# Column-major edge tiles in a chain of four modulated convolutions, with the edge products, edge tables and first iterations reordered

## The chip, the cores and the metric

One core of a Trainium2 chip runs the kernel. The metric is the device time of one execution in microseconds, as the median of several runs.

## The reference

The input x has 128 rows of 64 channels and 1024 positions. Four layers follow each other, each a 3-tap convolution whose weights are scaled for every row by a style vector, and the result is added to x. Layers 0 and 2 keep the length, layer 1 doubles it and blurs, layer 3 blurs and halves it.

```python
def _layer(x, style, w, b, mw, mb, typ):
    s = style @ mw.T + mb
    weight = SCALE * w * s[:, None, :, None]
    demod = lax.rsqrt(jnp.sum(weight * weight, axis=(2, 3)) + EPS)
    weight = weight * demod[:, :, None, None]
    if typ == 'same':
        out = jax.vmap(_conv_same)(x, weight) + b[None, :, None]
    elif typ == 'upsample':
        out = jax.vmap(_conv_up)(x, weight.transpose(0, 2, 1, 3)) + b[None, :, None]
        out = _blur(out, 2.0 * blur_k, (1, 1))
    elif typ == 'downsample':
        xb = _blur(x, blur_k, (2, 2))
        out = jax.vmap(_conv_down)(xb, weight) + b[None, :, None]
    return out
...
for i, typ in enumerate(TYPES):          # same, upsample, same, downsample
    out = _layer(out, style, weights[i], biases[i], mod_w[i], mod_b[i], typ)
x = x + out
```

## The kernel before

Away from the two ends of a row, the four layers and the blurs are one 9-tap convolution with weights of the row's own. The kernel computes these 9 x 64 x 64 weights for each row and then applies them. It works on four rows at a time ("quad" q, 32 of them); the array of TensorE is used as four quarters of 64 x 64, so that a step is four matmuls, each in two passes (float32).

Weights of a quad: stage1 (tile S, PSUM psS), stage2 (tile R, psR) and stage3 (tile Wf, PSUM psA or psW) are small products; between them ScalarE or VectorE copies the PSUM out with a factor from a table for the row (tA, tB, tBn, tC, t0). stage1 is split in stage1_a and stage1_b from quad 4 on: stage1_a computes three blocks, two "ends" and one "middle"; four copies take them to S; GpSimd adds and subtracts (L473, L474); stage1_b writes more blocks to the same PSUM and VectorE makes the rest of S (L483). The middle products of neighbouring rows are shared (share, share_copy: ScalarE copies the shared block into psR, L533, before stage2 of the next quad).

Convolution: x comes as three planes, and the 9 taps are computed as five products of 3 taps each, 342 columns wide (L816, 12 matmuls, 24 records of the profile): conv3, conv1, conv2, conv4, conv0. Their inputs T are sums and differences of planes (VectorE L763, L714 G and L794, GpSimd L780 and L785), their weights H are sums of the taps (VectorE L714 H, L711). conv3, conv1, conv2 and conv0 use the PSUM tile psA of the quad, conv4 the tile Y. VectorE takes psA into Y and y between them (L714, L873), ScalarE writes the outputs o (L893), and SP's queue stores them. psA has two buffers: open_a(q + 1), whose first user is stage3_b, takes the buffer of psA[q - 1].

Ends: the first and last three positions of a row don't follow the 9-tap rule. They are computed for all rows at once, layer by layer, from x's ends (Xe): the edge tiles Xm, Ye, Ue, Ve, We and Oe hold, for two ends (or halves) and 64 rows (HB), 3 to 6 positions each. Before, a row's positions are neighbours in memory. ends_matmul (L1046) multiplies such a tile with the weights of a layer, into the PSUM tile psA[q - 1], free at that time; rest0 to rest3 on VectorE (L1076, L1099, L1129, L1160) read it into the next edge tile with a table's factor. This happens in turns q = 10, 11, 13 and 24 (SLOTS), ahead of conv2(q). The factors (s0h, a0r, c0r, a1h, c1h, b1h, Dar, c2r, times) and the bias terms (add0, rest1_inner, add2) are made by GpSimd, a few in each turn (TABLES).

The order on every engine is the order in which the code is written (manual schedule): a prologue, early_turn for q = 0 to 3, turn_of for q = 4 to 28, then the last three quads by hand. In early_turn, q = 3 prepares two quads ("twice"); q = 4 is the first turn_of ("entry"). SMALL adds tiny matmuls (L1323) into columns of Y that small_zeros clears first (memset L1316). POOL in the profile is GpSimd, DVE VectorE, ACT ScalarE, PE TensorE.

Of the kernel before, what the change touches and what calls it, by code (L numbers as in the profile page):

```python
# [55 lines left out]
K = 3  # L56
# [7 lines left out]
def kernel(  # L64
# [395 lines left out]
    def stage1_a(q, ps=None):  # L460
# [532 lines left out]
    Xm = const.tile([P, 2, HB, K], F32, name="Xm")  # L993
# [11 lines left out]
    def zeros():  # L1005
        for t in (Ve, We):
            for s in range(2):
                nc_g.memset(t[:, s, :, 5:6], 0.0)
# [31 lines left out]
    def ends_matmul(ps, n, moving, plan):  # L1040
        for i, (weight, src, dst) in enumerate(plan):
            for r, rows in enumerate(HALF):
                for c, cols in enumerate(HALF):
                    out_ = ps[r][cols, : HB * n].rearrange("c (b j) -> c b j", j=n)
                    d = dst(r) if callable(dst) else dst
                    nc.tensor.matmul(  # L1046
                        out_[:, :, d],
                        weight(r, c)[rows],
                        moving[rows, c, :, src],
# [5 lines left out]
    def in_psum(t, n):  # L1055
        return t[:, :, : HB * n].rearrange("c h (b j) -> c h b j", j=n)
# [18 lines left out]
    def rest0(t):  # L1075
        nc_v.tensor_tensor(Ye[:, :, :, 1:], in_psum(t, K), spread(a0r, K), op=ALU.mult)  # L1076
# [51 lines left out]
    def rest2(t):  # L1128
        nc_v.tensor_tensor(Ve[:, :, :, :5], in_psum(t, 5), spread(Dar, 5), op=ALU.mult)  # L1129

    def add2():
        dst = Ve[:, :, :, :2]
        nc_g.tensor_add(dst, dst, spread(c2r, 2))

    def blur_side(part, i):
# [3 lines left out]
            dst[:, :, bs, :5], src[:, :, bs, :5], src[:, :, bs, 1:], op=ALU.add  # L1139
# [17 lines left out]
    def rest3(t):  # L1157
        scale = td.rearrange("c q r -> c (q r)")[:, :, None].to_broadcast([P, HB, K])
        for e in range(2):
            nc_v.scalar_tensor_tensor(  # L1160
                Oe[:, :, e], in_psum(t, K)[:, e], 0.125, scale, op0=ALU.mult, op1=ALU.mult
# [190 lines left out]
    def last_factors():  # L1352
        for i, f in enumerate((2.0, -1.0, 3.0)):
# [6 lines left out]
        7: lambda: table_b(REST),  # L1360
        8: lambda: of_half(s0h, sc[:, 0]),
        9: lambda: (
            nc_g.tensor_mul(quads(a0r), by_half(dm[:, 1]), by_half(dm[:, 0])),
            nc_g.tensor_copy(quads(c0r), by_half(c0f)),
        ),
# [406 lines left out]
```

## Time and profile before

| | |
|---|---|
| median of 3 runs | 468.58 us (468.55 to 469.73) |
| the profiled execution, device time | 468.84 us |
| its span, first to last instruction | 467.0 us |
| TensorE busy | 461.9 us, 99% |
| VectorE busy | 426.4 us, 91% |
| ScalarE busy | 329.6 us, 71% |
| GpSimd busy | 195.7 us, 42% |
| mean granted TensorE clock | 0.999 of full speed |
| HBM | 35.03 MB read, 34.01 MB written |

The profile is one execution, 1.8 us of which lie around the span. A row of the timeline gives the start and length in us, engine, line of the kernel, operation, tiles written and read, shape and count, and in brackets the idle time before it with what ended that. Matmuls overlap, and their ends are modelled, so their rows overlap too and TensorE looks busy where it waits briefly.

### The profile page before, as it was taken

The page shows a single profiled execution, that of the slowest core. Times are in us where ns is not written, and L with a number is a line of the kernel's source. Part 1 is how long each engine was busy: PE and PEld are TensorE (multiplying, and loading weights), DVE is VectorE, ACT ScalarE, POOL GpSimd, SP SyncE. Part 2 cuts the span into 40 slices and gives each one's busy share as a digit, 9 for nine tenths or more (in the row PEclk, how much of TensorE's full clock was granted, in tenths as well). Part 3 has the DMA queues.
Part 4 walks back from the last instruction along what each step waited for, and adds up shares of the span by engine and source line. Part 5 has one row for each costly group of instructions (what it writes and reads, how often), then busy time and mean ns, then how long its engine had stood idle before and what let it go on. Part 6 is the DMA issues. An engine that isn't in the chain of part 4 may idle for free.

```text
span 467.0 us, 26805 instructions
## 1 busy us (share of the span) xinstructions
PE 461.9 (99%) x11906; PEld 387.2 (83%) x11906; DVE 426.4 (91%) x671; ACT 329.6 (71%) x817; POOL 195.7 (42%) x263
## 2 busy tenths in 40 slices
PE   9999999999999999999999999999999999999996
PEld 6988789878777777998997777778777899998973
DVE  4989998889999999899899999999999899999995
ACT  4576667688777778576887777787777687776554
POOL 4733233676455535444333434423343433445410
PEclk9999999999999999999999999999999999999999
DMA  5226555425444534455344545444454534454225
GB/s 179 95 94 202 157 155 180 155 98 182 153 154 155 185 121 159 126 162 179 124 154 139 170 156 185 152 152 143 152 173 156 182 117 159 147 182 156 94 93 185
DMA packets 52837, 70.78 MB, mean 152 GB/s; under 512 B 6129, under 2 KB 50929, under 8 KB 52721
## 3 DMA queue, kind: packets, MB, share of 16 engines
q1 hardware_dynamic: 52496, 68.84, 45.6%
q8 instruction: 93, 1.52, 1.4%
q14 instruction: 24, 0.19, 0.2%
q10 hardware_dynamic: 224, 0.23, 0.1%
HBM read 35.03 MB, written 34.01 MB: 148 GB/s over the span
## 4 chain that ended last, share of the span: by engine, by line
PE 96%; DVE 2%; issue 0%; ACT 0%; DVEq 0%
PE psA L816 46%; PE Y L816 12%; PE psR L513 10%; PE psA L623 7%; PE psW L623 7%; PE psS L430 5%; PE psR L591 4%; PE psA L513 1%; PE psA L1046 1%; PE Y L184 1%; DVE G L714 0%; DVE H L714 0%; PE Y L380 0%; ACT S L400 0%; PE psM L221 0%
## 5 line engine op out<-in xcount | busy, mean ns | idle before, releaser
L816 PE MATMUL psA<-T,H 64*64 64x342 f32 x2304 | 191.9, 449 | 0.0
L816 PEld LDWEIGHTS psA<-T,H 64*64 64x64 f32 x2304 | 107.9, 134 | 32.6 <-issue 1.0
L780 POOL TENSOR_TENSOR T<-G 128x688 f32<-128x688 f32 x28 | 47.0, 1677 | 77.9 <-DVE G L714 71.4
L714 DVE SCALAR_TENSOR_TENSOR G<-X 128x1378 f32<-128x1378 f32 (+2 forms) x65 | 78.4, 1212 | 0.1
L816 PE MATMUL psA<-T,Wf 64*64 64x342 f32 (+1 forms) x918 | 67.6, 404 | 0.0
L473 POOL TENSOR_TENSOR S<-S 128x128 f32<-128x128 f32 x28 | 14.3, 511 | 127.1 <-ACT S L400 127.1
L816 PE MATMUL Y<-T,Wf 64*64 64x342 f32 x768 | 63.7, 448 | 0.0
L400 ACT ACTIVATE psW<-psA 128x128 f32<-128x128 f32 x100 | 19.4, 269 | 53.3 <-PE psA L623 51.2
L794 DVE TENSOR_TENSOR T<-G 128x1376 f32<-128x1376 f32 (+1 forms) x34 | 52.1, 1532 | 0.0
L763 DVE TENSOR_TENSOR T<-X 128x688 f32<-128x688 f32 x32 | 51.1, 1596 | 0.0
L400 ACT ACTIVATE Wf<-psW,t 128x256 f32<-128x256 f32 (+2 forms) x76 | 32.7, 479 | 25.4 <-PE psW L623 24.6
L400 ACT ACTIVATE R<-psR,tC 128x448 f32<-128x448 f32 x63 | 36.5, 630 | 18.0 <-PE psR L591 12.8
L785 POOL TENSOR_TENSOR T<-G 128x688 f32<-128x688 f32 x28 | 48.0, 1714 | 0.0
L816 PEld LDWEIGHTS psA<-T,Wf 64*64 64x64 f32 x918 | 42.8, 133 | 4.6 <-issue 0.2
L816 PEld LDWEIGHTS Y<-T,Wf 64*64 64x64 f32 x768 | 37.3, 133 | 10.5 <-DVE Y L714 0.2
L430 PEld LDWEIGHTS psS<-wd,w2n 64*64 64x64 f32 x1344 | 37.9, 134 | 8.3 <-ACT S L400 1.0
L893 ACT ACTIVATE o<-psA,tb,td 128x342 f32<-128x342 f32 x63 | 36.9, 641 | 5.2 <-PE psA L816 5.2
L714 DVE SCALAR_TENSOR_TENSOR Y<-m,psA 128x684 f32<-128x684 f32 x31 | 27.1, 874 | 14.4 <-PE psA L816 14.1
L714 DVE SCALAR_TENSOR_TENSOR H<-Wf 128x384 f32<-128x384 f32 x64 | 39.5, 618 | 0.0
L893 ACT ACTIVATE o<-y,tb,td 128x342 f32<-128x342 f32 x62 | 39.1, 694 | 0.0
L513 PE MATMUL psR<-S,E 64*64 64x64 f32 (+1 forms) x1152 | 39.0, 235 | 0.0
L513 PEld LDWEIGHTS psR<-S,E 64*64 64x64 f32 x1152 | 36.9, 134 | 2.5 <-ACT psR L533 0.3
(193 smaller groups left out, 922.9 us busy)
## 6 DMA issues: line engine op xcount, KB each, us to landing
out<-o SPq DMA_DIRECT2D x191, 172.0 KB, 2.1
X<-in_x SPq DMA_DIRECT2D x150, 172.0 KB, 3.3
X<-in_x SPq DMA_DIRECT2D x14, 516.0 KB, 4.6
par<-in_params SPq DMA_DIRECT2D x3, 192.0 KB, 3.4
Xe<-in_x_ends SPq DMA_DIRECT2D x1, 192.0 KB, 2.8
out<-o ACTq DMA_DIRECT2D x1, 172.0 KB, 1.9
par<-in_params SPq DMA_DIRECT2D x1, 160.0 KB, 2.7
out<-Oc SPq DMA_DIRECT2D x1, 150.0 KB, 1.7
```

Source lines behind the costliest of these rows:

```text
L400: nc_a.activation(dst, src, AF.Copy, scale=f)
L430: nc.tensor.matmul(ps[r][cols, at * C : (at + n) * C], weight[rows], wd[c if r == 0 else 1 - c][rows, taps], start=first, stop=last, skip_ ...
L513: nc.tensor.matmul(dst[r][cols], weight[rows], st[c if r == 0 else 1 - c][rows, slots, :], start=False, stop=last, skip_group_check=True,)
L591: nc.tensor.matmul(ps[r][cols, lo * C : (lo + m) * C], E[rows, e + 2, :], src[rows, a, :], start=(n == 0), stop=(n == 8), skip_group_check ...
L623: nc.tensor.matmul(dst[r][cols], weight[rows], t[rows, c, slots, :], start=first, stop=last, skip_group_check=True,)
L714: nc_v.scalar_tensor_tensor(out, x, f, y, op0=ALU.mult, op1=op)
L763: nc_v.tensor_sub(t[:, pairs, 0, :NJ], plane(X, 3, pairs), plane(X, 1, pairs))
L780: eng.tensor_add(t[:, :, 0, :NJ], plane(g, 2), plane(g, 1))
L785: eng.tensor_sub(t[:, :, 1, :NJ], plane(g, 2), plane(g, 1))
L794: nc_v.tensor_sub(t[:, pairs, :, :NJ], both(a, PL), both(b, 1))
L816: nc.tensor.matmul(ps[s][cols, at], w, Ts[q, tag][rows, c, i, g + at.start : g + at.stop], start=(g == at.start == 0 and (m == 3 or alone) ...
L893: nc_a.activation(dst, src, AF.Identity, bias=add, scale=d3)
```

## The change

1. Edge tiles and the PSUM that the edge products write are laid out position by position (for each position, 64 rows in a line) where they were row by row. The instructions and their sizes stay.
2. In turns 10, 11, 13 and 24 the edge products stand behind the first two of three tap groups of conv2, not ahead of it.
3. From turn 7 on, GpSimd makes the edge tables behind the two S operations of the turn (BEHIND_S), not ahead of them; s0h moves from turn 8 to 7 and c1h from 10 to 9.
4. First iterations: at q = 1 small_zeros stands ahead of in1 and in2, and in_g01(c) behind stage1_b; at q = 3 and 4 the two copies of stage1's middle block go from ScalarE to VectorE (stage1_middle), at q = 4 later than the ends' copies.

TensorE at the edge products of turn 11 (Ye and g, weights of layer 1) and at stage3_b behind conv2, with the engines whose semaphores each row waits for; before:

```order
L513 MATMUL psR_1_3553<-S_3203,E 64x64 x2
L1046 MATMUL psA_3097<-Ye,g_166 64x64x2 [waits Activation_49]
L1046 MATMUL psA_3097<-Ye,g_166 64x64x2 x11
L1046 MATMUL psA_3097<-Ye,g_166 64x64x2 [waits Pool_49]
L1046 MATMUL psA_3097<-Ye,g_166 64x64x2 x3
L1046 MATMUL psA_3097<-Ye,g_166 64x64 x8
L816 MATMUL psA_3388<-T_11_3287,H_3099 64x342 [waits DVE_49]
L816 MATMUL psA_3388<-T_11_3287,H_3099 64x342 x11
L623 MATMUL psA_3689<-R_3636,w0s_155 64x192 [waits DVE_49,Activation_49]
```

and after:

```order
L519 MATMUL psR_1_3553<-S_3201,E 64x64 x2
L822 MATMUL psA_3385<-T_11_3289,H_3097 64x342 [waits DVE_49,Pool_49]
L822 MATMUL psA_3385<-T_11_3289,H_3097 64x342 x7
L1053 MATMUL psA_3095<-Ye,g_166 64x2x64 [waits Activation_49]
L1053 MATMUL psA_3095<-Ye,g_166 64x2x64 x11
L1053 MATMUL psA_3095<-Ye,g_166 64x2x64 [waits Pool_49]
L1053 MATMUL psA_3095<-Ye,g_166 64x2x64 x3
L1053 MATMUL psA_3095<-Ye,g_166 64x64 x8
L822 MATMUL psA_3385<-T_11_3289,H_3097 64x342 x4
L629 MATMUL psA_3686<-R_3636,w0s_155 64x192 [waits DVE_49,Activation_49]
```

Between the edge products and stage3_b's first row there were 12 matmuls of conv2, and there are 4. That row waits for VectorE (DVE) before and after; in turns without edge products it waits for ScalarE alone.

GpSimd from turn 8 to 10 (S: stage1's sums, T: conv1's and conv2's inputs, R: stage2's sums, then the tables); before:

```order
L333 TENSOR_SCALAR s0h<-sc 64x64 x2
L473 TENSOR_TENSOR S_2928<-S_2928 128x2x64
L474 TENSOR_TENSOR S_2928<-S_2928 128x2x64
L780 TENSOR_TENSOR T_10_3012<-G_2942 128x2x344
L640 TENSOR_TENSOR R_3070<-R_3070 128x2x128
L785 TENSOR_TENSOR T_10_3012<-G_2942 128x2x344
L1363 TENSOR_TENSOR a0r<-dm 128x128
L1364 COPY c0r<-c0f 128x128
L473 TENSOR_TENSOR S_3203<-S_3203 128x2x64
L474 TENSOR_TENSOR S_3203<-S_3203 128x2x64
L780 TENSOR_TENSOR T_11_3287<-G_3217 128x2x344
```

and after:

```order
L481 TENSOR_TENSOR S_2928<-S_2928 128x2x64
L786 TENSOR_TENSOR T_10_3012<-G_2942 128x2x344
L646 TENSOR_TENSOR R_3070<-R_3070 128x2x128
L791 TENSOR_TENSOR T_10_3012<-G_2942 128x2x344
L480 TENSOR_TENSOR S_3201<-S_3201 128x2x64
L481 TENSOR_TENSOR S_3201<-S_3201 128x2x64
L1371 TENSOR_TENSOR a0r<-dm 128x128
L1372 COPY c0r<-c0f 128x128
L333 TENSOR_SCALAR c1h<-cc_152 64x64 x2
L786 TENSOR_TENSOR T_11_3289<-G_3215 128x2x344
```

The tables of a turn went from ahead of the S rows to behind them, ahead of the T row of conv1.

VectorE in iteration q = 1 (memset of small_zeros, conv1's and conv2's inputs, and so on to G of the next quad); before:

```order
L780 TENSOR_TENSOR T_2_952<-G_928 128x2x344
L785 TENSOR_TENSOR T_2_952<-G_928 128x2x344
L1316 MEMSET Y 128x16
L794 TENSOR_TENSOR T_2_1005<-G_928 128x1376
L763 TENSOR_TENSOR T_3_1007<-X_103 128x688
L985 TENSOR_TENSOR cc_152<-Y,a_145 128x16
L988 SCALAR_TENSOR_TENSOR cc_152<-b1s,cc_152 128x16
L714 SCALAR_TENSOR_TENSOR y_2_1072<-psA_989,m_2_1002 128x684
L714 SCALAR_TENSOR_TENSOR G_1074<-X_103 128x2x689
L483 SCALAR_TENSOR_TENSOR S_1049<-psS_0_1035,tB,S_1049 128x192
L483 SCALAR_TENSOR_TENSOR S_1049<-psS_1_1036,tB,S_1049 128x192
L714 SCALAR_TENSOR_TENSOR G_1074<-X_103 128x2x344
```

and after:

```order
L1323 MEMSET Y 128x16
L786 TENSOR_TENSOR T_2_955<-G_928 128x2x344
L791 TENSOR_TENSOR T_2_955<-G_928 128x2x344
L800 TENSOR_TENSOR T_2_1005<-G_928 128x1376
L769 TENSOR_TENSOR T_3_1007<-X_103 128x688
L991 TENSOR_TENSOR cc_152<-Y,a_145 128x16
L994 SCALAR_TENSOR_TENSOR cc_152<-b1s,cc_152 128x16
L720 SCALAR_TENSOR_TENSOR y_2_1072<-psA_990,m_2_1003 128x684
L489 SCALAR_TENSOR_TENSOR S_1049<-psS_0_1035,tB,S_1049 128x192
L489 SCALAR_TENSOR_TENSOR S_1049<-psS_1_1036,tB,S_1049 128x192
L720 SCALAR_TENSOR_TENSOR G_1104<-X_103 128x2x689
L720 SCALAR_TENSOR_TENSOR G_1104<-X_103 128x2x344
```

The memset went two rows up, and the two S rows stand ahead of the first G row.

The diff, cut to its core (the edge tiles' other index changes follow the same pattern):

```diff
-    def stage1_a(q, ps=None):
+    def stage1_a(q, ps=None, middle_by=nc_a):
...
+        chain[q] = wd, ps, st, t
+        if middle_by is not None:
+            stage1_middle(q, middle_by)
+
+    def stage1_middle(q, eng):
+
+        wd, ps, st, t = chain[q]
         for r in range(2):
             middle = ps[r][:, None, 7 * C : 8 * C].to_broadcast([P, 2, C])
-            scaled_copy(nc_a, st[r][:, 5:8:2, :], middle, tBn[:, q, r : r + 1])
+            scaled_copy(eng, st[r][:, 5:8:2, :], middle, tBn[:, q, r : r + 1])
         nc_g.tensor_add(t[:, :, 6], t[:, :, 0], t[:, :, 4])
         nc_g.tensor_sub(t[:, :, 6], t[:, :, 6], t[:, :, 5])
-        chain[q] = wd, ps, st, t
...
-    Xm = const.tile([P, 2, HB, K], F32, name="Xm")
+    Xm = const.tile([P, 2, K, HB], F32, name="Xm")
...
-    Ye = const.tile([P, 2, HB, 4], F32, name="Ye")
-    Ue = const.tile([P, 2, HB, 6], F32, name="Ue")
-    Ve = const.tile([P, 2, HB, 6], F32, name="Ve")
-    We = const.tile([P, 2, HB, 6], F32, name="We")
+    Ye = const.tile([P, 2, 4, HB], F32, name="Ye")
+    Ue = const.tile([P, 2, 6, HB], F32, name="Ue")
+    Ve = const.tile([P, 2, 6, HB], F32, name="Ve")
+    We = const.tile([P, 2, 6, HB], F32, name="We")
...
-                    out_ = ps[r][cols, : HB * n].rearrange("c (b j) -> c b j", j=n)
+                    out_ = ps[r][cols, : HB * n].rearrange("c (j b) -> c j b", j=n)
...
-                        out_[:, :, d],
+                        out_[:, d],
                         weight(r, c)[rows],
-                        moving[rows, c, :, src],
+                        moving[rows, c, src],
...
-        7: lambda: table_b(REST),
-        8: lambda: of_half(s0h, sc[:, 0]),
+    }
+    BEHIND_S = {
+        7: lambda: (table_b(REST), of_half(s0h, sc[:, 0])),
         9: lambda: (
             nc_g.tensor_mul(quads(a0r), by_half(dm[:, 1]), by_half(dm[:, 0])),
             nc_g.tensor_copy(quads(c0r), by_half(c0f)),
+            of_half(c1h, cc[0]),
         ),
-        10: lambda: (add0(), of_half(a1h, a1), of_half(c1h, cc[0])),
+        10: lambda: (add0(), of_half(a1h, a1)),
...
         if q == 1:
+            small_zeros(q)
             in1(n, nc_v)
             in2(n, nc_v)
...
-        small_zeros(q)
+        if q > 1:
+            small_zeros(q)
...
-        if q == 1:
-            in_g01(c)
         conv0(q, 1)
         if twice:
-            stage1_a(s)
+            stage1_a(s, middle_by=nc_v)
+            extra(q, 1)
...
         if q == 1:
+            in_g01(c)
             in_g2(c)
...
             if q - 1 in SLOTS:
+                conv2(q, 0, 1)
                 SLOTS[q - 1][0](banks(q - 1))
-            conv2(q)
+                conv2(q, 2)
+            else:
+                conv2(q)
...
-            stage1_a(s)
+            stage1_a(s, middle_by=None)
...
         in_g2(c)
+        if entry:
+            stage1_middle(s, nc_v)
+        side(BEHIND_S, q)
         side(AHEAD_OF_S, q)
```

More of the change, by code (lines that the diff above doesn't have):

```diff
@@ L1007, in zeros @@
             for s in range(2):
-                nc_g.memset(t[:, s, :, 5:6], 0.0)
+                nc_g.memset(t[:, s, 5], 0.0)
         for i in range(6):
@@ L1034, in setup_x @@
         s0 = spread(both_ends(s0h), K)[:, h]
-        nc_v.tensor_tensor(Xm[:, h], Xe[:, h], s0, op=ALU.mult)
+        src = Xe[:, h].rearrange("c b j -> c j b")
+        nc_v.tensor_tensor(Xm[:, h], src, s0, op=ALU.mult)
     def setup1(part):
@@ L1075, in rest0 @@
     def rest0(t):
-        nc_v.tensor_tensor(Ye[:, :, :, 1:], in_psum(t, K), spread(a0r, K), op=ALU.mult)
+        nc_v.tensor_tensor(Ye[:, :, 1:], in_psum(t, K), spread(a0r, K), op=ALU.mult)
     def add0():
-        nc_g.tensor_add(Ye[:, :, :, 0], Ye[:, :, :, 1], c0r)
+        nc_g.tensor_add(Ye[:, :, 0], Ye[:, :, 1], c0r)
     def ends1(ps):
@@ L1128, in rest2 @@
     def rest2(t):
-        nc_v.tensor_tensor(Ve[:, :, :, :5], in_psum(t, 5), spread(Dar, 5), op=ALU.mult)
+        nc_v.tensor_tensor(Ve[:, :, :5], in_psum(t, 5), spread(Dar, 5), op=ALU.mult)
     def add2():
-        dst = Ve[:, :, :, :2]
+        dst = Ve[:, :, :2]
         nc_g.tensor_add(dst, dst, spread(c2r, 2))
@@ L1444, in early_turn @@
                 of(PART[1])
+        for i in range(2):
+            output(q, 2, i)
         if q == 1:
+            small_zeros(q)
             in1(n, nc_v)
             in2(n, nc_v)
-        for i in range(2):
-            output(q, 2, i)
         if late(q):
```

16 lines of the change are left out of this document (7 added, 9 removed).

## The prediction

> **What bounds the kernel now.** I read the page's first part and its chain of waits, then the table of busy time for single turns of the loop.
>
> ```profile
> span 467.0 us, 26805 instructions
> ...
> PE 461.9 (99%) x11906; PEld 387.2 (83%) x11906; DVE 426.4 (91%) x671; ACT 329.6 (71%) x817; POOL 195.7 (42%) x263
> ...
> PE 96%; DVE 2%; issue 0%; ACT 0%; DVEq 0%
> ```
>
> Each window below is one turn, from one second-stage start to the next; behind its length stand the busy times of PE, PEld, DVE, ACT and POOL.
>
> ```profile
> 141.96:155.91 13.95, 13.95 (x386) 11.14 (x384) 13.68 (x21) 10.58 (x28) 6.25 (x7) 1.00 0.50 159
> 155.91:169.87 13.96, 13.96 (x386) 10.75 (x384) 13.36 (x20) 10.46 (x28) 6.11 (x7) 1.00 0.49 156
> 169.87:184.29 14.42, 14.42 (x411) 11.23 (x409) 13.22 (x21) 10.41 (x28) 8.25 (x10) 1.00 0.46 147
> 184.29:199.77 15.48, 15.48 (x434) 14.62 (x432) 13.66 (x21) 10.41 (x28) 7.07 (x8) 1.00 0.43 139
> ...
> 213.64:228.98 15.34, 15.34 (x418) 14.86 (x418) 13.77 (x20) 10.84 (x29) 6.23 (x6) 1.00 0.43 138
> 270.26:284.00 13.74, 13.74 (x387) 10.68 (x385) 13.13 (x20) 10.47 (x28) 4.96 (x5) 1.00 0.50 158
> 366.34:381.30 14.96, 14.96 (x419) 13.30 (x414) 13.24 (x21) 10.49 (x28) 5.58 (x5) 1.00 0.47 147
> ```
>
> TensorE is the bound: 99% busy, 96% of the chain. Its matmuls' ends are modelled, so a short stall looks busy; the length of a turn shows it instead. A plain turn (270.26) takes 13.74 us; turns 8 and 9 take 0.21 and 0.22 more; the edge turns (q = 10, 11, 13 and 24, from 169.87, 184.29, 213.64 and 366.34) take 0.68, 1.74, 1.60 and 1.22 more, 5.24 in all. VectorE has 13.13 of 13.74 in a plain turn, so it has little room either.
>
> **Term 1: edge tiles column-major.** Groups by shape (count, then busy us, mean ns of one):
>
> ```profile
> L513 PE MATMUL psR<-S,wsq 64*64 64x128 f32 x576 | 30.2, 271 | 0.0
> ...
> L513 PE MATMUL psR<-S,wsq 64*64 64x64 f32 x768 | 27.5, 217 | 0.0
> ...
> L1046 PE MATMUL psA<-We,par 64*64 64x128 f32 x24 | 1.5, 339 | 0.0
> ...
> L1046 PE MATMUL psA<-Ye,g 64*64 64x128 f32 x32 | 1.1, 273 | 0.0
> ...
> L1046 PE MATMUL psA<-Ye,g 64*64 64x64 f32 x16 | 0.7, 286 | 0.0
> L1046 PE MATMUL psA<-Ue,par 64*64 64x128 f32 x8 | 0.7, 332 | 0.0
> ...
> L1046 PE MATMUL psA<-We,par 64*64 64x64 f32 x8 | 0.5, 287 | 0.0
> ```
>
> Three pieces of the chain of waits (start, us, what):
>
> ```profile
> 56.44 2.68 PE psR L591 x53
> ...
> 71.66 2.50 PE psR L591 x64
> ...
> 272.48 1.73 PE psA L816 x24
> ```
>
> A record is one of two passes of a matmul, and four quarters of the array work side by side. An L816 product of 24 records of 342 columns takes 1.73 us: 72 ns a record, 0.21 ns per column. The edge products stream 3072, 5120, 6144 and 3584 columns (Xm, Ye, Ue, We): at that rate 3.8 us together. Their turns pay 5.24, so 1.45 is waste at most. From the other side: single columns of Ye, Ue and We, 6 to 4 elements apart, last some 287 ns against 217 of a plain 64x64, and pairs of Ue and We some 335 against 271. With four records to a pass that is 4 × 69 (Ye) + 2 × 61 + 2 × 70 (Ue, its singles taken as We's) + 6 × 68 + 2 × 70 (We) = 1.1 us. Column-major makes every column 64 neighbours, as in L513. I take **-1.3** (bounds -1.1 and -1.45).
>
> The Trainium skill (SBUF — State Buffer, section "Door 1: The DMA port swizzle (why `[64,N]` ≈ `[32,N]`)") says SBUF runs at full rate with two accesses to a 16-byte line, and any non-contiguous PSUM pattern slows matmuls. The trace agrees with the first and not with the second: Ye's pairs write PSUM 4 elements apart and last 273 ns against 271. By the second, Ye's 8 pair passes would gain too, some 0.5, and term 1 would be -1.8; I take the row.
>
> **Term 2: edge products behind two thirds of the third product.** The VectorE step that reads the edge PSUM (rest0 to rest3), and its place in turn 11:
>
> ```profile
> 173.33 0.55 DVE L1076 TENSOR_TENSOR Ye<-psA,a0r 128x384 f32<-128x384 f32 x1
> ...
> 186.36 1.55 PE L1046 MATMUL psA<-Ye,g 64*64 64x128 f32 x47
> ...
> 188.04 0.96 DVE L1099 TENSOR_TENSOR Ue<-psA,a1h 128x768 f32<-128x768 f32 x1 [0.16 <-PE psA L1046]
> ...
> 217.73 0.82 DVE L1129 TENSOR_TENSOR Ve<-psA,Dar 128x640 f32<-128x640 f32 x1 [0.25 <-PE psA L1046]
> ...
> 369.99 0.62 DVE L1160 SCALAR_TENSOR_TENSOR Oe<-psA,td 128x192 f32<-128x192 f32 x2 [0.20 <-PE psA L1046]
> ```
>
> The first matmul of stage3_b writes the PSUM tile that the edge products used, and in these four turns alone its row in the order waits for VectorE: for this read. Today a whole third product (1.73 us) covers it: in turn 11 the edge matmuls end at 187.91, the read starts 0.13 later and is over at 189.00, long enough before stage3_b. In the new order only 8 records (8 × 72 ns = 0.58) cover it. After the last edge matmul is issued, its result is 0.16 away (217 ns less one 55 ns step), VectorE starts 0.13 later, reads for R, and TensorE resumes some 0.1 after that (0.15 in a row below, at 50.81): stall = 0.16 + 0.13 + R + 0.1 - 0.58 = R - 0.19. The read's length goes with its elements (384: 0.55, 768: 0.96) and these stay. So 0.36, 0.77, 0.63 and 0.43: **+2.2** (bounds 0, if something covers it yet, and 2.4). The sum on VectorE behind the read (Y) is needed only after stage3_b, so it costs nothing more.
>
> **Term 3: the first iterations.** Rows of the timeline at q = 1 (from 49.84), q = 3 (from 84.46) and q = 4 (from 96.30):
>
> ```profile
> 49.84 0.80 PE L816 MATMUL psA<-T,Wf 64*64 64x342 f32 x8
> ...
> 50.59 0.07 DVE L1316 MEMSET Y<- 128x16 f32 x1
> ...
> 50.81 0.23 PE L1323 MATMUL Y<-c0f,wsum 64*64 64x16 f32 x2 [0.17 <-DVE Y L1316]
> ...
> 84.46 0.90 PE L816 MATMUL psA<-T,H 64*64 64x342 f32 x8
> 85.24 0.76 PE L430 MATMUL psS<-wd,w2n 64*64 64x64 f32 x22
> ...
> 86.11 0.42 DVE L483 SCALAR_TENSOR_TENSOR S<-psS,tB,S 128x192 f32<-128x192 f32 x1 [1.01 <-PE psS L430]
> ...
> 96.30 0.53 PE L430 MATMUL psS<-wd,w2n 64*64 64x64 f32 x24
> ...
> 97.38 0.81 PE L816 MATMUL psA<-T,H 64*64 64x342 f32 x8
> 98.12 0.77 PE L430 MATMUL psS<-wd,w2n 64*64 64x64 f32 x22
> ...
> 98.98 0.42 DVE L483 SCALAR_TENSOR_TENSOR S<-psS,tB,S 128x192 f32<-128x192 f32 x1 [1.28 <-PE psS L430]
> ```
>
> q = 1: the 8 records from 49.84 are issued by 50.42, but the next matmul starts at 50.81, 0.15 after the memset's end: 0.39 lost. With the memset two products earlier the wait goes; about half is lost again, since y on VectorE stands where it stood and is late next. S ahead of G (two places up) then frees the next second stage, 2.68 in the chain against 2.50: 0.2. Together -0.4. q = 3: 84.46 + 0.58 is 85.04, L430 starts at 85.24, and lasts 0.76 against 0.53: 0.4 of waiting for all four copies on ScalarE, of which two go to VectorE. q = 4: 97.38 + 0.58 against 98.12, and 0.77 against 0.53: 0.4 in the same way, but there Newton steps stand behind the copies on VectorE, so I count 0.2. The copies on VectorE (two of 128 elements; nearest row 0.47 for two of 64, below) are covered by its idle 1.01 and 1.28; without that cover they would cost 0.5 a turn. **-1.0** (bounds 0, if VectorE or ScalarE is late anyway, and -1.3).
>
> **Term 4: edge tables later on GpSimd.** The timeline at turn 9, and at the same step of a plain turn and the plain turn's end:
>
> ```profile
> 161.69 0.83 POOL L1363 TENSOR_TENSOR a0r<-dm 128x128 f32<-128x128 f32 x1
> ...
> 162.07 0.77 DVE L711 SCALAR_TENSOR_TENSOR Wf<-idn,t,Wf 128x64 f32<-128x64 f32 x2
> ...
> 276.47 0.47 DVE L711 SCALAR_TENSOR_TENSOR Wf<-idn,t,Wf 128x64 f32<-128x64 f32 x2
> ...
> 283.25 0.57 ACT L533 COPY psR<-psA 128x192 f32<-128x192 f32 x2 [0.23 <-DVE S L483]
> ...
> 284.00 0.51 PE L513 MATMUL psR<-S,E 64*64 64x128 f32 x14
> ```
>
> Beside a GpSimd table L711 takes 0.77, alone 0.47: the tables hold VectorE up in its chain to H, and turns 8 and 9 are 0.2 longer. Behind the S sums they meet G and S (L483) instead; from there ScalarE's psR copy ends at 283.82, 0.18 ahead of the next second stage. One table of 0.3 to 0.8 in front of G would thus give back much of it. Turn 8 loses its tables to turn 7, the others about break even: **-0.2** (bounds -0.7, all waste of turns 7 to 14 gone, and +2.0, the third rival). The remaining VectorE edits (layout of Xm to Oe) move as many elements as before and cost nothing, hidden or not. No transfer is moved: SP's order is the same.
>
> **Sum.** -1.3 + 2.2 - 1.0 - 0.2 = -0.3 us. The profiled execution took 468.84 (span 467.0 and 1.8 around it), 0.26 above the median of 468.58; it would become 468.5, the median **468.3**. About 0.3% (1.4 us) is what a measurement of this kernel can tell from no change.
>
> **Rivals.** First, the stall of term 2 does not come: the profile lists no wait of stage3_b, and VectorE idles before Y in edge turns; but the order has that wait. Then 468.3 - 2.2 = 466.1. Second, column-major does not do its part, since the 287 ns come from the order of the products and not from spacing: +1.3, 469.6; against it, Ye's pairs and singles differ in spacing within one run of products. Third, slower: GpSimd tables hold VectorE up twice on the way to S in turns 7 to 14. With two tables of 0.3 to 0.45 in six turns and less in one, less 0.15 of room a turn, and the waste of today's turns regained, that is some +2.0: 470.3. It decides when a table in front of G and one in front of S are both waited for; L711 doubles for it, but L483 reads PSUM, and no run of it beside a table is in the trace. The Trainium skill (SBUF — State Buffer, section "SBUF: two separate sides") has this as an exclusive lock, taken for a whole instruction by GpSimd or by a VectorE operation with two SBUF inputs; by that rule G waits and L483 does not, which gives the forecast's term 4 rather than this rival.
>
> **How the numbers follow.** Forecast 0.56 (467.2 to 469.4; 0.08 of it below 467.2), no stall 0.20, no gain from the layout 0.12, slower 0.12. Faster by over 0.3%: 0.20 + 0.08 = 0.28; within: 0.48 + 0.12 = 0.60; slower: 0.12. The range, 465.9 to 469.7, takes in the first two rivals and leaves out the third and the first's lower edge.
>
> **What would show it.** Edge groups at 217 and 271 ns (term 1); edge turns with waits "PE or PEld psA <- DVE" of 0.4 to 0.8 and lengths near 14.8, 15.6, 15.7 and 14.9 (term 2); no L1323 wait at 50, and L430 at 0.53 in q = 3 and 4 (term 3); turn 8 at 13.74, turns 9 and 12 a little over (term 4). I am wrong if the edge turns fall to 13.74 plus their columns, or if plain turns change.

## The result, and the profile after

The changed kernel takes 472.34 us (median of 6 runs, 471.69 to 472.78) against 469.08 (468.35 to 469.79) for the kernel before on the same chip: a ratio of 1.0068, 95% interval 1.0052 to 1.0084, some 3.2 us slower. The prediction was 468.3, range 465.9 to 469.7, with a chance of 0.12 for slower. It was wrong.

The page of the changed kernel (a profiled execution with a span of 470.3 us, before 467.0), busy time and chain:

```profile
PE 462.4 (98%) x11906; PEld 376.9 (80%) x11906; DVE 428.7 (91%) x675; ACT 328.1 (70%) x813; POOL 203.9 (43%) x263
...
PE 95%; DVE 3%; issue 1%; ACT 1%; POOL 0%; DVEq 0%; ACTq 0%
```

TensorE has 0.5 us more of busy time in a span 3.3 us longer, and VectorE now holds 3% of the chain: TensorE waits. Where is seen by turn (changed kernel; columns as before):

```profile
70.86:87.48 16.62, 15.62 (x344) 12.06 (x336) 15.18 (x29) 12.15 (x28) 5.95 (x10) 1.00 0.50 161
87.48:100.90 13.42, 13.42 (x330) 10.40 (x332) 11.93 (x24) 6.29 (x17) 9.78 (x17) 1.00 0.36 105
100.90:115.03 14.13, 14.13 (x392) 12.13 (x388) 13.44 (x21) 11.76 (x31) 9.18 (x11) 1.00 0.54 173
142.98:157.46 14.48, 14.32 (x387) 11.10 (x384) 14.34 (x21) 10.57 (x28) 7.58 (x7) 1.00 0.47 154
157.46:171.17 13.71, 13.71 (x386) 10.23 (x382) 13.11 (x20) 10.13 (x27) 6.94 (x9) 1.00 0.49 155
171.17:186.28 15.11, 14.83 (x411) 11.93 (x411) 14.21 (x21) 10.95 (x30) 8.62 (x9) 1.00 0.44 143
186.28:202.02 15.74, 15.07 (x434) 12.41 (x430) 13.41 (x21) 10.26 (x28) 7.74 (x9) 1.00 0.43 138
215.81:231.89 16.08, 15.54 (x418) 12.41 (x418) 13.84 (x20) 11.04 (x30) 6.05 (x6) 1.00 0.42 133
369.40:384.45 15.05, 14.74 (x419) 12.10 (x415) 13.13 (x21) 10.53 (x29) 5.37 (x5) 1.00 0.47 146
```

These are turns 3, 4, 5, 8, 9, 10, 11, 13 and 24. The table has the lengths of the turns that differ, from second stage to second stage, in one profiled execution of each kernel (computed from the starts, so the last digit can differ by one from a row). The columns after the second are experiments, described below; bold marks the turns for which each is read:

| turn | before | changed | edges first | edges after one group | q = 3 on ScalarE | oc ahead | oc ahead, tA behind | tables as before | layout alone | layout alone, 128 records later | combined |
|---|---|---|---|---|---|---|---|---|---|---|---|
| 1 | 14.64 | 14.23 | 14.25 | 14.29 | 14.29 | 14.28 | 14.29 | 14.28 | 14.65 | 14.60 | 14.28 |
| 2 | 15.09 | 14.99 | 14.99 | 15.01 | 15.02 | 15.01 | 15.02 | 15.00 | 15.10 | 15.10 | 15.02 |
| 3 | 15.61 | 16.62 | 16.62 | 16.61 | **15.48** | **15.65** | **15.35** | 16.61 | 15.61 | 15.61 | 15.48 |
| 4 | 13.22 | 13.42 | 13.42 | 13.42 | 13.14 | 13.14 | 13.19 | 13.42 | 13.22 | 13.22 | 13.22 |
| 5 | 13.87 | 14.13 | 14.13 | 14.13 | 14.12 | 14.12 | 14.12 | 14.12 | 13.86 | 13.86 | 13.87 |
| 8 | 13.95 | 14.48 | 14.52 | 14.49 | 14.50 | 14.51 | 14.50 | **14.02** | 14.01 | 14.00 | 14.02 |
| 9 | 13.96 | 13.71 | 13.72 | 13.69 | 13.71 | 13.71 | 13.72 | **14.02** | 14.03 | 14.01 | 13.72 |
| 10 | 14.41 | 15.10 | **14.61** | **14.60** | 15.11 | 15.10 | 15.11 | **14.82** | 14.35 | 14.83 | 14.61 |
| 11 | 15.48 | 15.75 | **15.27** | **16.27** | 15.75 | 15.75 | 16.17 | 15.92 | **15.95** | **14.97** | 14.98 |
| 13 | 15.34 | 16.08 | **15.02** | **15.50** | 16.08 | 16.01 | 16.09 | 16.16 | 15.00 | 15.00 | 15.19 |
| 24 | 14.96 | 15.05 | **14.46** | **14.48** | 15.05 | 15.31 | 15.06 | 15.03 | 14.47 | 15.31 | 14.47 |

From the first turn to the last the changed kernel is 3.27 us longer: turns 1 and 2 -0.51, turn 3 +1.01, turns 4 and 5 +0.46, turns 8 and 9 +0.28, the four edge turns +1.79. The remaining 0.24 (turns 21 to 23 and 28 above all) I did not trace.

The edge products by shape, after:

```profile
L1053 PE MATMUL psA<-Ye,g 64*64 64x128 f32 x32 | 1.1, 269 | 0.0
L1053 PE MATMUL psA<-We,par 64*64 64x128 f32 x24 | 1.0, 270 | 0.0
...
L1053 PE MATMUL psA<-Ye,g 64*64 64x64 f32 x16 | 0.5, 218 | 0.0
```

They last what the plain products of their size last (271 and 217), where We's pairs took 339 and Ye's singles 286. The price of their new place stands in the timeline, here around turn 11's edge products and the end of turn 24's (start, length; in brackets idle time):

```profile
190.55 0.45 PE L822 MATMUL psA<-T,H 64*64 64x342 f32 x1
190.58 0.23 PE L1053 MATMUL psA<-Ye,g 64*64 64x64 f32 x2
190.61 0.78 PE L822 MATMUL psA<-T,H 64*64 64x342 f32 x7
192.06 0.56 PE L629 MATMUL psA<-R,w0s 64*64 64x192 f32 x8 [0.67 <-DVE Ue L1106]
...
190.95 0.96 DVE L1106 TENSOR_TENSOR Ue<-psA,a1h 128x768 f32<-128x768 f32 x1 [1.31 <-PE psA L1053]
...
373.34 0.83 PE L822 MATMUL psA<-T,H 64*64 64x342 f32 x8
374.48 0.56 PE L629 MATMUL psA<-R,w0s 64*64 64x192 f32 x8 [0.31 <-DVE Oe L1167]
```

The eight records of conv2 that are left need 0.58 us. In turn 11 stage3_b starts 1.51 after the first of them, in turn 24 1.14 (turns 10 and 13, read in the same way: 1.07 and 1.34). The loss is 0.49, 0.93, 0.76 and 0.56: 2.74 us. VectorE starts 0.40 after the first of those records, reads for 0.96, and TensorE goes on 0.15 later.

Turn 3 on VectorE and GpSimd, before:

```profile
84.86 0.23 DVE L982 TENSOR_SCALAR oc<-oc,par_s 128x16 f32<-128x16 f32 x1
...
86.00 1.66 POOL L780 TENSOR_TENSOR T<-G 128x688 f32<-128x688 f32 x1
```

and on VectorE, GpSimd and TensorE, after:

```profile
84.10 0.61 DVE L402 TENSOR_SCALAR S<-psS,tBn 128x128 f32<-128x128 f32 x2 [0.41 <-ACT S L400]
...
85.17 0.17 DVE L987 TENSOR_TENSOR oc<-Y,dm 128x16 f32<-128x16 f32 x1
85.38 1.73 DVE L988 TENSOR_SCALAR oc<-oc,par_s 128x16 f32<-128x16 f32 x1
87.02 0.73 DVE L489 SCALAR_TENSOR_TENSOR S<-psS,tB,S 128x192 f32<-128x192 f32 x2
...
85.42 1.65 POOL L786 TENSOR_TENSOR T<-G 128x688 f32<-128x688 f32 x1
...
84.51 0.63 PEld L430 LDWEIGHTS psS<-wd,w2n 64*64 64x64 f32 x22 [0.35 <-DVE S L402]
84.56 0.71 PE L430 MATMUL psS<-wd,w2n 64*64 64x64 f32 x22
...
87.48 0.78 PE L597 MATMUL psR<-S,E 64*64 64x192 f32 x10 [1.00 <-DVE S L489]
```

An operation on 16 elements (L988, the bias oc) takes 1.73 us, from just before the start of GpSimd's conv1 input to its end; before, it took 0.23. The S operation stands behind it, and TensorE waits for S. The change put it there: with the copies it also moved `extra(q, 1)`, the operations on tA and oc, from ahead of conv0's second group to behind the copies, which the diff above shows only by its added line. L988 now starts 14.52 us into the turn, before 13.52; GpSimd's conv1 input starts at 14.56, before 14.66.

Turn 8, s0h on GpSimd before:

```profile
148.05 1.13 POOL L333 TENSOR_SCALAR s0h<-sc 64x64 f32<-64x64 f32 x2
```

and GpSimd and VectorE after:

```profile
142.59 2.15 POOL L333 TENSOR_SCALAR s0h<-sc 64x64 f32<-64x64 f32 x2
144.82 2.32 POOL L786 TENSOR_TENSOR T<-G 128x688 f32<-128x688 f32 x1
...
142.50 1.58 DVE L720 SCALAR_TENSOR_TENSOR G<-X 128x1378 f32<-128x1378 f32 x1
...
145.56 1.80 DVE L1037 SCALAR_TENSOR_TENSOR g<-par,g 128x192 f32<-128x192 f32 x1
```

The first of the two operations of s0h starts 0.09 after VectorE's G and ends at 144.31, 0.23 after it; conv1's input starts late, and VectorE's g (2.8 us for its four instances in the profile, so 0.35 for each of the others) ends 0.21 after that input.

### The profile page after: what moved, and what is told of

Same layout as the page of the kernel before. It is cut to its first block, busy times and chain, and to the rows that moved or that the text cites. A ratio compares the mean times of both kernels' runs of the same rounds, so it can differ in the third digit from the quotient of the medians.

```text
span 470.3 us, 26802 instructions
## 1 busy us (share of the span) xinstructions
PE 462.4 (98%) x11906; PEld 376.9 (80%) x11906; DVE 428.7 (91%) x675; ACT 328.1 (70%) x813; POOL 203.9 (43%) x263
## 4 chain that ended last, share of the span: by engine, by line
PE 95%; DVE 3%; issue 1%; ACT 1%; POOL 0%; DVEq 0%; ACTq 0%
PE psA L822 46%; PE Y L822 11%; PE psR L519 10%; PE psW L629 7%; PE psA L629 7%; PE psS L430 5%; PE psR L597 4%; PE psA L519 1%; PE psA L1053 1%; PE Y L184 1%; PE Y L380 0%; PE psM L221 0%; DVE g L1037 0%; DVE H L720 0%; ACT S L400 0%
## 5 line engine op out<-in xcount | busy, mean ns | idle before, releaser
L822 PEld LDWEIGHTS psA<-T,H 64*64 64x64 f32 x2304 | 103.0, 133 | 34.7 <-issue 1.2
L480 POOL TENSOR_TENSOR S<-S 128x128 f32<-128x128 f32 x28 | 17.1, 611 | 138.9 <-ACT S L400 138.9
L822 PE MATMUL psA<-T,Wf 64*64 64x342 f32 (+1 forms) x918 | 66.6, 404 | 0.0
L822 PEld LDWEIGHTS psA<-T,Wf 64*64 64x64 f32 x918 | 41.8, 133 | 4.8 <-issue 0.2
L822 PEld LDWEIGHTS Y<-T,Wf 64*64 64x64 f32 x768 | 35.3, 133 | 12.1 <-DVE Y L720 0.2
L430 PEld LDWEIGHTS psS<-wd,w2n 64*64 64x64 f32 x1344 | 36.3, 134 | 9.5 <-DVE S L402 0.8
L519 PE MATMUL psR<-S,E 64*64 64x64 f32 (+1 forms) x1152 | 40.6, 236 | 0.0
L519 PE MATMUL psR<-S,wsq 64*64 64x64 f32 (+1 forms) x1344 | 39.4, 240 | 0.0
```

The costliest lines, as they stand in the source:

```text
L430: nc.tensor.matmul(ps[r][cols, at * C : (at + n) * C], weight[rows], wd[c if r == 0 else 1 - c][rows, taps], start=first, stop=last, skip_ ...
L519: nc.tensor.matmul(dst[r][cols], weight[rows], st[c if r == 0 else 1 - c][rows, slots, :], start=False, stop=last, skip_group_check=True,)
L822: nc.tensor.matmul(ps[s][cols, at], w, Ts[q, tag][rows, c, i, g + at.start : g + at.stop], start=(g == at.start == 0 and (m == 3 or alone) ...
```

## The experiments

Four theories were on record beside their rivals: the stall at stage3_b costs 2.75 us; turn 3's loss is oc's operation beside GpSimd's long one; turn 8's loss is the tables' new place; and later, that TensorE runs out of instructions.

**Edges first.** Column-major tiles stay, the edge products go ahead of conv2 again.

```diff
-                conv2(q, 0, 1)
                 SLOTS[q - 1][0](banks(q - 1))
-                conv2(q, 2)
-            else:
-                conv2(q)
+            conv2(q)
```

> The changed kernel with the edge products back ahead of the whole third product; column-major tiles and all else stay. Theory (the read on VectorE stands between the edge products and stage3_b, and 8 records of conv2 cover only 0.58 us of it; 0.50, 0.92, 0.77 and 0.57 us were lost in turns 10, 11, 13 and 24): 2.75 us less than the changed kernel, 469.6 us or a ratio to the kernel before of 1.001, the last 8 records of conv2 at 0.58 us again, turns 10, 11, 13 and 24 at about 14.5, 14.8, 15.1 and 14.5 us. Rival (only the 2.2 us of the forecast are the stall, the rest of the longer edge turns comes from the tables on GpSimd): 2.2 us less, 470.1 us, and turns 10, 11 and 13 stay 0.2 above the lengths just given. Rival (the edge turns are long for another reason, the order of GpSimd's tables): the time stays at 472.3.

Measured: 469.79 us, ratio 1.0005 (0.9991 to 1.002). The four edge turns, windows of this run:

```profile
171.58:186.19 14.61, 14.61 (x410) 12.22 (x410) 13.74 (x21) 10.80 (x29) 8.69 (x9) 1.00 0.46 148
186.19:201.46 15.27, 15.27 (x434) 14.34 (x430) 13.66 (x21) 10.33 (x28) 8.03 (x9) 1.00 0.45 141
215.35:230.37 15.02, 15.02 (x419) 14.95 (x416) 13.61 (x20) 10.72 (x29) 6.27 (x6) 1.00 0.46 145
367.76:382.22 14.46, 14.46 (x419) 13.19 (x414) 13.16 (x21) 10.50 (x28) 5.59 (x5) 1.00 0.47 152
```

They are 0.49, 0.48, 1.06 and 0.59 shorter, 2.62 in all: the theory's size, and the greater part of the whole slowdown. That the sum fits is in part luck: turn 11 gave back only half of its 0.93 (the runs with the layout alone show why), and turn 13 gave back 0.30 more than its 0.76, because work behind its second stage begins 2.02 us into the turn here and at 2.31 in the changed kernel.

**Edges after one group**, run twice (`conv2(q, 0)`, the edge products, `conv2(q, 1, 2)`), so that 16 records cover the hand-over.

> The changed kernel with the edge products behind one of the three tap groups of conv2, so that 16 records (1.16 us) and not 8 (0.58) stand between them and stage3_b. Theory (the stall is the hand-over to VectorE, its read and the hand-over back, less what conv2 covers): the stalls of 0.50, 0.92, 0.77 and 0.57 become 0, 0.34, 0.19 and 0: 2.2 us less than the changed kernel, 470.1 us, ratio 1.002. Rival (VectorE's read is late for a reason of its own in these turns, so that it moves with the edge products): no more than 1 us less, ratio 1.0045 or above.

472.09 us, ratio 1.0052 (1.0033 to 1.0071). One of its seven executions took 1708 us, and it was the profiled one, so it was run again:

> The changed kernel with the edge products behind one of the three tap groups of conv2, a second time (the first run's one profile took 1706 us and can't be read). Theory: 16 records and not 8 stand between the edge products and stage3_b, so the stalls of 0.50, 0.92, 0.77 and 0.57 become 0, 0.34, 0.19 and 0, and turns 10, 11, 13 and 24 go from 15.10, 15.75, 16.08 and 15.05 to 14.6, 15.2, 15.5 and 14.5: 2.2 us less. Rival (VectorE's read is late for a reason of its own, so that it moves with the edge products; the first run's 472.09 us speaks for this): these turns get at most 0.25 shorter each.

471.81 us, ratio 1.0048 (1.0029 to 1.0067). The windows of the same four turns:

```profile
171.67:186.28 14.61, 14.61 (x411) 12.02 (x409) 13.71 (x21) 10.68 (x29) 8.71 (x9) 1.00 0.48 149
186.28:202.55 16.27, 15.62 (x434) 12.73 (x432) 14.13 (x21) 10.65 (x29) 7.47 (x9) 1.00 0.43 133
216.36:231.86 15.50, 15.50 (x418) 12.45 (x418) 14.13 (x20) 11.05 (x30) 6.07 (x6) 1.00 0.44 138
369.39:383.87 14.48, 14.48 (x419) 12.75 (x415) 13.21 (x21) 10.49 (x28) 5.60 (x5) 1.00 0.48 152
```

Turns 10, 13 and 24 come out as the theory said (14.6, 15.5, 14.5); turn 11 is 1.1 longer than it said, so that the median moved by less than 1 us and not by 2.2. The hand-over is confirmed, and something else in turn 11 is not in it.

**q = 3 on ScalarE**: `stage1_a(s, middle_by=nc_v)` becomes `stage1_a(s)`.

> The changed kernel with the two copies of stage1's middle block at q = 3 back on ScalarE; on VectorE the small operations on tA and oc keep their order. Theory (at q = 3 VectorE with the copies comes to the small oc operation only when GpSimd has begun conv1's input, and stands beside it for 1.73 us; S and the next second stage are late by that): turn 3 goes from 16.62 us to about 15.6, 1.0 us less than the changed kernel, 471.3 us, ratio 1.0047; the oc operation lasts 0.23 us again. Rival (the turn is longer because the second stage of that turn meets something else, such as q = 1's new order): turn 3 stays within 0.3 of 16.62.

470.87 us, ratio 1.0025 (1.001 to 1.004). Turn 3 is 15.48, oc's operation 0.23 us. Turns 4 and 5, where the copies are still on VectorE, are 13.14 and 14.12 against 13.22 and 13.87 before: that half of the step loses 0.2 by itself.

**oc ahead.** The copies stay on VectorE, with `extra(q, 1)` (tA and oc) ahead of them, behind `sum1(n)` as in the kernel before.

> The changed kernel with the copies of q = 3 still on VectorE, but the small operations on tA and oc ahead of them, where they stood in the kernel before. Theory (the loss of turn 3 is that oc's operation falls beside GpSimd's long input operation, not the time of the copies): oc's operation lasts about 0.23 us, S starts within 0.3 of the time at which the middle copies allow it, turn 3 goes from 16.62 to 15.4 to 15.7 us, 1.0 less than the changed kernel, 471.3 us. Rival (the copies themselves, 0.6 us on VectorE, are what makes S late): turn 3 stays above 16.1 us.

471.08 us, ratio 1.0034 (1.0018 to 1.005); turn 3 15.65. Its timeline on VectorE:

```profile
86.09 0.23 DVE L988 TENSOR_SCALAR oc<-oc,par_s 128x16 f32<-128x16 f32 x1
86.23 0.60 DVE L402 TENSOR_SCALAR S<-psS,tBn 128x128 f32<-128x128 f32 x2
87.50 0.74 DVE L489 SCALAR_TENSOR_TENSOR S<-psS,tB,S 128x192 f32<-128x192 f32 x2 [0.66 <-PE psS L430]
```

The copies last the same 0.6 us here, and S starts 14.81 into the turn (16.16 in the changed kernel, 14.77 before). So it is oc's place that cost 1 us, not the copies.

**oc ahead, tA behind.** Only the oc operations move ahead of the copies.

```diff
-        (3, 1): lambda: (table_A(REST, dm[:, 2, REST]), small_rest(3)),
+        (3, 1): lambda: table_A(REST, dm[:, 2, REST]),
...
         sum1(n)
+        if q == AHEAD:
+            small_rest(3)
```

> The changed kernel, copies of q = 3 on VectorE, with the two small oc operations ahead of the copies, in the 0.41 us in which VectorE waited for ScalarE there, and tA behind them. Theory (only the oc operation's place beside GpSimd's long operation made turn 3 long): oc 0.2 us each, S about 1.6 us earlier in the turn, turn 3 at 15.2 to 15.5 us, 1.2 us less than the changed kernel, 471.1 us, ratio 1.004; shorter by 0.1 to 0.3 than with the copies on ScalarE (15.48) or with tA ahead too (15.65). Rival (whatever small operation comes behind the copies is held up): tA is held instead, turn 3 stays above 16.2 us.

Turn 3 is 15.35, the shortest of all, oc 0.23: as the theory said. The time, 472.08 us, ratio 1.006 (1.0041 to 1.0079), is 1 us above what was expected. The profile shows 0.42 of that: turn 11 took 16.17, though nothing in it was changed.

**Tables as before.** TABLES as in the kernel before, ahead of the S operations; the rest of the change stays.

> The changed kernel with the edge tables ahead of the S operations as in the kernel before. Theory (two tables behind S at turn 7 hold VectorE up twice and cost turn 8 0.53 us, later turns gain 0.25 at turn 9 and lose little): turn 8 back to 13.95, turn 9 to 13.96 us, 0.3 less than the changed kernel, 472.0 us, ratio 1.006. Rival (the tables behind S are also behind the losses of turns 10, 11 and 13): these three turns get 0.2 to 0.5 shorter each, 1.0 less in all, 471.3 us. Rival (the move helps as its gain at turn 9 shows): 0.2 us more.

472.26 us, ratio 1.0057 (1.0039 to 1.0075). Turns 8 to 10:

```profile
142.57:156.59 14.02, 14.02 (x386) 11.17 (x384) 13.75 (x21) 10.58 (x28) 6.31 (x7) 1.00 0.50 159
156.59:170.61 14.02, 14.02 (x386) 10.75 (x384) 13.43 (x20) 10.46 (x28) 6.18 (x7) 1.00 0.49 156
170.61:185.43 14.82, 14.56 (x410) 11.56 (x408) 13.71 (x21) 10.64 (x28) 7.88 (x10) 1.00 0.45 141
```

Against these the tables behind S cost 0.46 in turn 8 and 0.28 in turn 10, and gain 0.31 in turn 9, 0.17 in turn 11 and 0.13 in turns 12 and 13: +0.13 in all, nothing that the time can show.

**Layout alone.** The kernel before with column-major tiles and PSUM, and nothing else.

> The kernel before with column-major edge tiles and PSUM and nothing else of the change. Theory (every column of an edge product then costs 0.21 us per 1000 ns of rows as in the plain products, and the order on no engine moves): turns 11, 13 and 24 shorter by 0.21, 0.32 and 0.50 us (as in the run with the edge products ahead), turn 10 as before, so about 1.0 us less than the kernel before, ratio 0.9978; the forecast's term was 1.3, ratio 0.9972. Rival (the layout makes VectorE's edge operations, whose rows are 64 elements now, or Xm's transposing multiplication slower and hides part of the gain): ratio 0.999 to 1.0.

468.83 us, ratio 0.9991 (0.9977 to 1.0005): less than either forecast. Turns 13 and 24 are 0.34 and 0.49 shorter, turn 10 0.06; turn 11 is 0.47 longer. Its timeline inside conv2 of turn 11, TensorE and its weight loads:

```profile
188.31 0.74 PE L822 MATMUL psA<-T,H 64*64 64x342 f32 x3
189.49 1.66 PE L822 MATMUL psA<-T,H 64*64 64x342 f32 x18 [0.43 <-issue]
...
189.48 1.06 PEld L822 LDWEIGHTS psA<-T,H 64*64 64x64 f32 x18 [1.03 <-issue]
```

No record starts for 0.88 us in the middle of a product, and no engine is named as the releaser. Counting all of TensorE's records in order of start, that is weight loads, matmuls and some 120 semaphore instructions, which the views leave out, the stop is at record 9409. The stop in turn 11 of the run with tA behind is at record 9665, exactly 256 later. The instruction queue moves blocks of 16384 bytes, 93 for the span's 23,936 records, some 256 each. Hence the last theory and its test:

**Layout alone, 128 and 256 records later.** Matmuls that add zeros to Y, in the prologue:

```diff
     zeros_to_y(2, 256, False)
+    for _ in range(8):          # 16 in the second kernel
+        zeros_to_y(2, 32, False)
```

> The column-major layout alone, with 64 more matmuls that add zeros to Y in the prologue, which put 128 more records (weight loads and matmuls) ahead of all that follows; the prologue may get longer by 1 to 3 us, so turn 11 is what is read. Theory (in turn 11 of the layout-alone run TensorE stops for 0.88 us in the middle of conv2 because its next 256 instructions are not there yet: the stop lies at record 9409, in another run with the same stop at 9665, 256 later, and it ends 1.5 us after a transfer of 16384 bytes in the instruction queue; the 256 records ahead of it are the stage2 and edge products, all short): the border between two blocks of 256 now falls in the middle of stage2 and no stop comes in conv2; turn 11 at 14.8 to 15.1 us against 15.95, no gap over 0.3 us between TensorE's records there. Rival (the stop is a wait on another engine, ended by GpSimd's R sum, which ends 0.06 before TensorE goes on): the stop stays at the same instruction of conv2, turn 11 stays above 15.6.

> The same with 128 more matmuls, 256 records, so that the borders between blocks of 256 fall on the same instructions of the loop as without any. Theory (the block that holds turn 11's stage2 and edge products takes as long as its successor takes to arrive: 0.5 to 0.6 us until the transfer starts, 0.9 to 1.6 for it, 1.2 to 1.5 more): turn 11 at 14.9 to 16.0 us, depending on that transfer, and where it is over 15.2 the lost time lies at the same matmul of conv2 as in the layout-alone run, record 9665. Rival (the added matmuls change something else in turn 11): it comes out as with 64 more, below 15.1, though the transfer takes over 1.3 us.

Each was run once (471.54 and 472.01 us, with a longer prologue); the turns are what is read. With 128 more records (turns 10, 11, 13 and 24, and the place in turn 24's conv2):

```profile
172.60:187.43 14.83, 14.66 (x411) 13.54 (x408) 13.63 (x21) 10.60 (x28) 7.53 (x10) 1.00 0.45 141
187.43:202.39 14.96, 14.96 (x436) 14.16 (x431) 13.91 (x21) 10.30 (x28) 6.59 (x8) 1.00 0.47 148
216.19:231.20 15.01, 15.01 (x419) 14.77 (x417) 13.69 (x20) 10.74 (x29) 6.29 (x6) 1.00 0.45 141
368.56:383.88 15.32, 15.17 (x419) 14.04 (x415) 13.11 (x21) 10.49 (x28) 5.57 (x5) 1.00 0.45 142
```

Turn 11 falls from 15.95 to 14.97 and has no stop. Two stops appear elsewhere, of 0.44 in turn 10 and 0.60 in turn 24, which are now 0.48 and 0.84 longer than with the layout alone. Their records are 8897 and 19649: like 9409 and 9665 they are 193 more than a multiple of 256. With 256 more records turn 11 is 15.22, with a small stop (0.16) at record 9665, the same matmul as with none added. That is inside the theory's wide range and only 0.1 above the rival's, so this run by itself says little. The rival of the first run, a wait for GpSimd's R sum, would have stayed at its instruction when 128 records were added, and falls. The stops of turn 11 in the second run with the edges after one group (0.33 and 0.66, records 9409 and 9665) are of this kind and make up its missing 1 us. Smaller ones stand in turn 11 with the edges first (0.26, record 9409) and in turn 24 with oc ahead (0.26, record 19649).

**Combined.** Column-major tiles, edge products ahead of conv2, the new order at q = 1, copies at q = 3 and 4 on ScalarE, tables behind S from turn 9 on only.

> The kernel before with column-major edge tiles, the edge products ahead of the third product, the new order at q = 1, the copies at q = 3 and 4 on ScalarE, and the edge tables behind S from turn 9 on only (turns 7 and 8 as before). Theory (the parts add up: layout 0.8 to 1.0 less in turns 10 to 24, q = 1 and 2 0.4 to 0.5, turn 9 0.25 less, turn 10 0.2 more): 1.3 to 1.7 us less than the kernel before, ratio 0.9965 to 0.997. Rival (the parts don't add up, because the order of GpSimd's tables takes back in turns 10 to 13 what the layout gives): ratio 0.9985 to 1.0.

468.05 us, ratio 0.9971 (0.9955 to 0.9986): the parts add up, at the smaller end of what was expected, and it beats both kernels. Its turn 11 met no stop in the profiled execution. The same with the copies of q = 3 on VectorE and oc ahead of them:

> The fastest version so far (column-major edge tiles, edge products ahead of conv2, new order at q = 1, edge tables behind S from turn 9 on), with the copies of q = 3 on VectorE, the oc operations ahead of them and tA behind them. Theory (turn 3 at 15.35 and turn 4 at 13.2, as with that order in the changed kernel, against 15.48 and 13.22): 0.15 us less, 467.9 us, ratio to the kernel before 0.9968, which can't be told from 0.9971. Rival (VectorE's copies cost something later): 468.3 or above.

468.53 us, ratio 0.9978 (0.9965 to 0.9991): where the rival put it, not the theory. Turn 3 is 15.35 as expected, and turn 11 met a stop of 0.41 at record 9409 in the profiled execution and took 15.43; but that execution was the fastest of the twelve (467.29 us), so the stop doesn't explain the median. The intervals overlap, and the two versions can't be told apart.

## Why the prediction was wrong, step by step

**Term 1, right in mechanism and nearly in size.** Predicted -1.3, bounds -1.1 and -1.45. The records' lengths came out as forecast, and without a stop the turns are 0.06, 0.51 (in the run with 128 records more), 0.34 and 0.49 shorter: -1.40. But only half of turn 11's 0.51 is the layout. The kernel before already stops at record 9409; its weight loads in turn 11:

```profile
188.18 1.06 PEld L816 LDWEIGHTS psA<-T,H 64*64 64x64 f32 x18 [0.30 <-issue]
```

Two of its weight loads start 0.45 apart there. In the run with 256 records more they start 0.45 apart as well, and its turn 11 is 0.26 shorter than that of the kernel before; that is the layout's part. So the layout gives -1.15, the smaller of the prediction's two sums (1.1), and the other 0.25 came to the changed kernel by luck: it met no stop in turn 11. What the prediction did not have is that turn 11's short products can run into the next block of instructions; the layout alone kept only some 0.4 of its gain.

**Term 2, mis-sized.** The stall came in all four turns, which rules out the first rival. Predicted +2.2, measured +2.74: the hand-over to VectorE took 0.36 to 0.40 from the first conv2 record where the sum had 0.29, and TensorE came back after 0.15 instead of 0.1. The prediction had the row with 0.15 in hand and took 0.1. With the other terms the edge turns come out: turn 10 is 14.41 + 0.49 + 0.28 (tables) - 0.06 = 15.12 (15.10), turn 11 15.48 + 0.93 - 0.51 - 0.17 = 15.73 (15.75), turn 24 14.96 + 0.56 - 0.49 = 15.03 (15.05). Turn 13 is 0.4 above such a sum, most of it from its second stage, which starts in pieces: against the layout alone, where the work behind the second stage begins 2.02 us into the turn and not 2.31, it closes, 15.00 + 0.29 + 0.76 = 16.05 (16.08). Why the second stage is late there I did not find.

**Term 3 is the step that failed.** Predicted -1.0, measured +0.96. q = 1 gave -0.51 with turn 2 where -0.4 was forecast: turn 1 got back all of its 0.39, not half. At q = 3 the prediction called the copies covered by VectorE's idle 1.01 us and did not ask what stood behind them on VectorE: tA and oc, which now came 1.0 us later (0.41 of waiting for ScalarE and 0.61 of copies), into GpSimd's long operation. That turned -0.4 into +1.01. The gain itself was too high as well: L430 was to fall to 0.53 and takes 0.71 at q = 3 and 0.76 at q = 4 (before 0.76 and 0.77), because it now waits 0.35 and 0.40 for VectorE's copies. In the right order the copies on VectorE are worth 0.13 (15.35 against 15.48), not 0.4. The Trainium skill (SBUF — State Buffer, section "SBUF: two separate sides") describes a port that a GpSimd operation, or a VectorE operation in a two-port mode or with two SBUF inputs, holds until it is done. The trace agrees with the hold: this oc operation, with one tensor from SBUF, took 0.23 us ahead of GpSimd's operation and 1.73 beside it; in which mode it ran no run shows. In turns 4 and 5 the step lost 0.46 where -0.2 was forecast; the run with q = 3 on ScalarE (27.26 for the two turns against 27.09 before) puts 0.2 of it down to the copies there, and the rest went away with turn 3's loss.

**Term 4, wrong in sign and small.** Predicted -0.2, +0.13 by the run with the tables as before. The third rival had GpSimd's tables hold VectorE up. What came is mostly the other way round: a short table operation that starts within 0.2 us of VectorE's G lasts about as long as G. It came four times, with s0h above (1.72 us), c1h at the end of turn 9 (1.82, the row below), a1h at the end of turn 10 (1.68) and the bias of Ue at the end of turn 11 (1.72), where b1h and a second s0h take 0.37 and that bias took 0.53 before.

```profile
170.90 1.82 POOL L333 TENSOR_SCALAR c1h<-cc 64x64 f32<-64x64 f32 x1
```

Time it cost in the turns behind two of them alone: 0.46 in turn 8, where GpSimd's late input then held VectorE's g, and 0.28 in turn 10. The rival's 470.3 came closer to 472.3 for another reason.

Between -0.3 and +3.27 lie 3.6 us: some 2.0 of them are term 3, 0.5 term 2 and 0.3 term 4, with 0.1 the other way from term 1 and turn 11's missing stop together; the remaining 0.8 are turn 13's 0.4 and the small differences of turns 8 to 28.

## What to carry to other kernels

When an operation is moved in front of others on an engine, follow everything behind it to the next long operation of the engine that shares its port: here 1.0 us of delay put a 0.2 us operation into a 1.7 us hold. Products whose PSUM is read by another engine before it is reused need that read, plus about half a microsecond for going and coming back, of independent matmuls behind them; count them before moving the products. And where many short matmuls stand together, look for gaps without a releaser at equal distances in the count of instructions before crediting a faster matmul with its time.

## What the runs showed of the hardware

The traces read as if TensorE's instructions came in blocks of 256 records, 16384 bytes each, and TensorE could be ahead of them. In thirteen profiles (all but that of 1708 us) there are seven gaps of over 0.3 us between TensorE's records, from turn 8 on, that no engine's work explains; all seven lie 193 records behind a multiple of 256 (semaphore instructions counted), and in all of them TensorE goes on 1.31 to 1.57 us after the end of the transfer in the instruction queue that precedes it. At no such border from turn 8 on, the last of each program left out, does it go on less than 1.20 us after that. Four follow a short block (stage2 and edge products one behind the other, 3.2 to 3.75 us with the stop), whose transfer began 0.5 to 0.7 us after the border; in the other three the transfer began only 3.5 to 3.75 us after the border, and why it was so late no run shows. Whether a stop comes varies: the combined kernel crossed the same border after 2.79 us without one. In the six profiles with column-major tiles and the edge products ahead of conv2, turn 11 takes longer the longer the pause between two weight loads at the border: 14.97 and 14.98 us without one, 15.22 at 0.45, 15.27 at 0.49, 15.43 at 0.65 and 15.95 at 1.17. The Trainium skill (Runtime: NRT & Kernel Launch, section "Instruction fetch mechanics") has the blocks of 16 KiB and 256 instructions, with which the trace agrees, and says that fetching is hidden by the pace of issue, which does not hold for these short matmuls.

The second thing is the price of a hand-over through PSUM: 0.36 to 0.40 us from TensorE's next record to VectorE's start and 0.15 back, in all four turns, beside the 0.56 to 0.96 of the read itself.
